# Gathers that wait for the gathers in front of them to be issued

## The chip, the cores and the metric

The kernel runs on one core of one Trainium2 chip. Its five engines are TensorE (PE, the matmuls; PEld is its weight load), VectorE (DVE), ScalarE (ACT), GpSimd (POOL) and SyncE (SP, which here only issues DMAs). The metric is the device time of one launch in microseconds; for a version of the kernel it is the median of several runs without a profiler. A profile is one more execution, taken with the hardware profiler on.

## What is computed

The reference is one layer of a graph network over B = 16 graphs of N = 1024 nodes with C = 64 channels. A node's new value comes from weighted quantiles, per channel, of its neighbours' values. Before that, a node with more than ten neighbours drops some of them.

```python
h = relu(layernorm(x))
neigh = (adj > 0) & ~eye
skip  = where(nb > 10, (nb + 1) // 2, 1)          # nb: number of neighbours
rem   = neigh & (skip > 1) & (rank % skip == skip - 1) & mask
rem   = rem | rem.T
nd    = (adj with its diagonal set, without rem) > 0
s     = sort(where(nd[..., None], h[None], inf), axis=neighbours)
agg   = sum of w * (quantile tau of s)             # tau .25, .5, .75; w .25, .5, .25
out   = h + agg
y     = relu(out @ W1 + b1) @ W2 + b2
x     = x + y * mask
```

The adjacency has about one edge in 128, so a node keeps few neighbours, and the kernel works on lists of them.

## The kernel before

A batch is one graph. `prepare(b)` makes its lists: `load` and `normalize` read the adjacency and the node values from HBM, `drop` and `keep` find on PE and ACT which edges stay, `order` sorts the nodes by their number of neighbours so that nodes with lists of like length lie in the same tile of 128 (eight tiles in four classes with 13, 11, 9 and 7 places), and `collect` leaves, on DVE, the index list `idx` of each tile. `normalize` also writes the node values to a table `htab` in HBM, one row of 64 values for each node.

`fetch(m, classes)` queues the gathers for a pair of batches m. A gather is one indirect DMA that GpSimd issues: for one place s of one tile it reads one index for each of the 128 partitions and brings 128 rows of `htab` to the tile `g` of its class. A pair has 126 of them, the eight pairs 1008; they all stand at line 1199. `fetch_group` adds 26 gathers (L1402) and 4 reads of rows of x (L1406) for the few nodes with long lists, `scatter` 4 indirect writes (L1445).

`aggregate(m)` then sorts the lists in `g` with min and max on DVE (L1236, L1237), weights them (L1244) and adds them up on PE in `acc` (L1246). `mlp` puts the sums in the nodes' order with one-hot matmuls and runs the two layers. `results(m)` is both.

The outer loop runs over m = 0 to 8. In each turn `weave` interleaves `results(m - 1)` with `prepare` for the batches 2m + 2 and 2m + 3 and takes queued gathers out with `issue` as the results advance. The classes with long lists have two buffers for `g`, the other two classes one: their gathers for the next pair can't run until the sums of this one are done.

The order of the program is not the order on the engines. At the end `arrange` takes all instructions, estimates what each costs (a POOL DMA 1330 ns and 950 ns more until its result), lays them out in time with a list schedule, and ties each engine to the order that comes out. Waits between engines are put in afterwards by the framework, one semaphore for each engine; the DMAs that GpSimd issues take eight semaphores in rotation for their completion, and as a rule a gather waits until the one that used its semaphore before has landed. [...] a further wait is put in a semaphore instruction in front of it on the same engine.

The lines that matter below: 1199 (the gather), 639 (`arrange`), 723 (where `arrange` writes the fixed order of each engine), 1175 (the queue and `issue`), 1542 (the call of `arrange`).

Of the kernel before, what the change touches and what calls it, by code (L numbers as in the profile page):

```python
# [635 lines left out]
        return 570, 1700 + by / 200  # L636


def arrange(tc, tails=()):

    steps, found, number = [], {}, {}
    for ins in list(tc.nc.cur_bb.bb.instructions):
        if type(ins).__name__.startswith("BassTile"):
            continue
        if ins.name in tails:
            at = found[tails[ins.name]]
            at.tail.append(ins)
            number[ins.name] = len(number)
            at.busy += Step(ins, 0).busy
            found[ins.name] = at  # L650
            continue
        found[ins.name] = Step(ins, len(steps))
        steps.append(found[ins.name])

    written, read, users, order = {}, {}, {}, {}
    for s in steps:
        for u in s.reads + s.writes:
            name = u.tile.name
            for o, other in written.get(name, ()):
                if u.meets(other):  # L660
                    s.before.add(o.place)
            if u in s.writes:
                for o, other in read.get(name, ()):
                    if u.meets(other):
                        s.before.add(o.place)
        for u in s.writes:
            for table in (written, read):
                table[u.tile.name] = [e for e in table.get(u.tile.name, ()) if not u.covers(e[1])]
            written[u.tile.name].append((s, u))
        for u in s.reads:  # L670
            read.setdefault(u.tile.name, []).append((s, u))
        for u in s.reads + s.writes:
            if getattr(u.tile, "tag", None):
                if u.tile.name not in users:
                    order.setdefault(u.tile.tag, []).append(u.tile)
                users.setdefault(u.tile.name, []).append(s)
    for tiles in order.values():
        for k, t in enumerate(tiles):
            bufs = t.tag_meta.bufs
            first = users[t.name][0]  # L680
            if k:
                first.behind.add(users[tiles[k - 1].name][0].place)
            if k >= bufs:
                first.before.update(o.place for o in users[tiles[k - bufs].name])
            for o in users[t.name][1:]:
                if o is not first:
                    o.before.add(first.place)
    for s in steps:
        s.behind -= s.before
        s.before.discard(s.place)  # L690
        s.behind.discard(s.place)
        s.left, s.ready = len(s.before) + len(s.behind), 0.0
        for p in (*s.before, *s.behind):
            steps[p].after.append(s)

    free = dict.fromkeys(ENGINES, 0.0)
    waiting, able, sequence = ({e: [] for e in ENGINES} for _ in range(3))
    for s in steps:
        if not s.left:
            heappush(waiting[s.engine], (0.0, s.place))  # L700
    for _ in steps:
        when, e = min(
            (free[e] if able[e] else max(free[e], waiting[e][0][0]), e) for e in ENGINES if able[e] or waiting[e]
        )
        while waiting[e] and waiting[e][0][0] <= when:
            heappush(able[e], heappop(waiting[e])[1])
        s = steps[heappop(able[e])]
        sequence[e].append(s)
        free[e] = when + s.busy
        for o in s.after:  # L710
            if s.place in o.behind:
                least = when
            else:
                least = free[e] + (s.lag + 60 if o.engine != e or s.moves else 115 if e == "DVE" else 0)
            o.ready = max(o.ready, least)
            o.left -= 1
            if not o.left:
                heappush(waiting[o.engine], (o.ready, o.place))
        for q in ENGINES:
            while waiting[q] and waiting[q][0][0] <= free[q]:  # L720
                heappush(able[q], heappop(waiting[q])[1])

    for steps in sequence.values():
        alike = iter(sorted((i for s in steps for i in s.tail), key=lambda i: number[i.name]))
        line = [i for s in steps for i in (s.ins, *(next(alike) for _ in s.tail))]
        for ins, then in zip(line, line[1:]):
            tc.add_manual_dep(
                then, ins.name, mybir.DependencyInfo(mybir.DependencyClass.NoSync, mybir.DependencyReason.DATA),
                reason="order of the engine",
            )  # L730
# [3 lines left out]
def list_layer(  # L734
# [14 lines left out]
    nc = tc.nc  # L749
# [420 lines left out]
    tails = {}  # L1170
# [2 lines left out]


    queue = deque()
    turn = [0]

    def issue(many=None):
# [8 lines left out]
    def fetch(m, classes=CLASSES, halves=(0, 1)):  # L1187

        for tiles, slots in classes:
            lo, n = tiles[0], len(tiles)  # L1190
            held, order = PLANS[slots][:2]

            def begin(h, tiles=tiles, lo=lo, n=n, slots=slots, held=held):
                if (m, tiles) not in gathered:
                    gathered[m, tiles] = wk.tile([P, held, n, 2, C], F32, name=f"g{lo}", bufs=2 - lo // 4)
                nc.scalar.copy(gathered[m, tiles][:, slots - 1, :, h], owns[m][:, lo:lo + n, h])

            def gather(h, slot, k, at, tiles=tiles, lo=lo):
                return nc.gpsimd.indirect_dma_start(  # L1199
                    out=gathered[m, tiles][:, slot, k - lo, h], out_offset=None, in_=tables[2 * m + h],  # L1200
                    in_offset=bass.IndirectOffsetOnAxis(ap=lists[2 * m + h][:, at:at + 1], axis=0),
                )

            for h in halves:
                queue.append(partial(begin, h))
                for k in tiles:
                    for s, slot in enumerate(order[:FULL[k] + ((k, FULL[k]) in HOSTS)]):
                        queue.append(partial(gather, h, slot, k, PASSED[k] + s))
# [68 lines left out]
    def aggregate(m, o):  # L1277
# [4 lines left out]
        for half in (0, 1) if last else (1, 0):  # L1282
# [30 lines left out]
            if half and not last:  # L1313
                fetch(m + 1, CLASSES[2:])
# [197 lines left out]
    late_constants()  # L1512
    drain(both(ahead, drop(0), normalize(0)), keep(0), order(0), collect(0, ((0, 1), (1, NT))))
    fetch(0, halves=(0,))
    issue()
    drain(load(1), prepare(1))
    fetch(0, halves=(1,))
    issue()
    for m in range(pairs + 1):
# [19 lines left out]
    fp = psum.tile([1, 1], F32, name="fp", tag="misc")  # L1539
    nc.tensor.matmul(fp, worst, ones_col(cst, nc), start=True, stop=True)  # L1540
    nc.vector.tensor_scalar(flag, fp, 0.0, None, OP.is_gt)
    arrange(tc, tails)


def ones_col(pool, nc):
# [68 lines left out]
@with_exitstack  # L1614
def quantile_graph_layer(
    ctx: ExitStack,
    tc: tile.TileContext,
    x: bass.AP,
    adj: bass.AP,
    nodemask: bass.AP,  # L1620
    W1: bass.AP,
    b1: bass.AP,
    W2: bass.AP,
    b2: bass.AP,
    cbf: bass.AP,
    cf32: bass.AP,
    ci32: bass.AP,
    out: bass.AP,
):
    keep = ctx.enter_context(tc.tile_pool(name="keep", bufs=1))  # L1630
    flag = keep.tile([1, 1], I32, name="flag")
    list_layer(tc, x, adj, nodemask, W1, b1, W2, b2, cbf, cf32, out, flag)
    full = tc.nc.values_load(flag[0:1, 0:1], min_val=0, max_val=1)
    with tc.If(full > 0):
        dense_layer(tc, x, adj, nodemask, W1, b1, W2, b2, cbf, cf32, ci32, out)
# [83 lines left out]
```

## Time and profile before

| | us |
|---|---|
| timed runs, median of 3 | 1597.93 (1597.37 to 1602.03) |
| profiled execution | 2649.33 |
| its span, first to last instruction | 2647.5 |
| PE busy, 8385 matmuls | 1188.3 |
| DVE busy, 3716 instructions | 1183.8 |
| ACT busy, 2510 instructions | 937.0 |
| POOL busy, 1047 instructions | 1029.6 |
| first gather starts / last gather starts | 92.0 / 2441.9 |
| mean granted TensorE clock, share of full speed | 0.69 |

A row of the groups reads: line, engine, operation, output and inputs, count, then busy us and the mean ns of one, then the idle time of the engine just before these instructions and what ended most of it. "issue" is a start that waited for nothing that the trace shows; "remote" is a wait whose releaser the trace does not know. In the timeline a row is start, duration, engine, line, operation, and in brackets the idle time before it. [...] The profiled execution of this kernel takes 1.66 times as long as a timed run, so a share of its span is not a share of the timed run.

### The profile page before, as it was taken

To read this page: it belongs to the slowest core of one execution; us is meant where nothing else is said; L and a number is where in the kernel's file an instruction comes from. 1 tells how busy PE (TensorE), PEld (TensorE's weight loads), DVE (VectorE), ACT (ScalarE), POOL (GpSimd) and SP (SyncE) were. 2 spreads that over 40 slices of the span, in tenths; PEclk is the share of its full clock that TensorE was granted. 3 is DMA by queue.
4 is the path that set the end of the run, shared out by engine and by line. 5 is a ranking of instruction groups with operands and counts; after the bars stand their busy time and mean duration, and the time that the engine had idled before them with its cause. 6 is when DMAs were issued, how large, how long until landed. Compare 5 with 4: busy or idle time off the path is not lost.

```text
span 2647.5 us, 25734 instructions
## 1 busy us (share of the span) xinstructions
PE 1188.3 (45%) x8385; PEld 719.3 (27%) x8385; DVE 1183.8 (45%) x3716; ACT 937.0 (35%) x2510; POOL 1029.6 (39%) x1047
## 2 busy tenths in 40 slices
PE   4427076253807481446616354444942463123235
PEld 2214043132404240223313232232521231021122
DVE  2303066232607460555319323495851452281883
ACT  6528075243607350536225252424631230001001
POOL 0442712744272437252550626307074626406000
PEclk9758577577957695677757676676965676556667
DMA  4323121222222211212111211302220101101000
GB/s 139 92 49 91 41 69 56 60 58 52 50 45 83 54 48 30 77 45 66 34 50 58 52 42 38 84 17 62 53 60 17 31 11 31 28 0 24 16 0 11
DMA packets 151250, 127.47 MB, mean 48 GB/s; under 512 B 117538, under 2 KB 118050, under 8 KB 151106
## 3 DMA queue, kind: packets, MB, share of 16 engines
q1 hardware_dynamic: 117762, 91.52, 12.3%
q0 software_dynamic: 33344, 34.21, 6.7%
q8 instruction: 68, 1.11, 0.2%
q14 instruction: 76, 0.62, 0.1%
HBM read 110.10 MB, written 13.81 MB: 47 GB/s over the span
## 4 chain that ended last, share of the span: by engine, by line
another core or an unknown queue 34%; PE 20%; ACT 16%; DVE 16%; issue 10%; DMA 2%; SPq 1%; DVEq 0%; POOL 0%; POOLq 0%; ACTq 0%
PE codeP L1041 5%; DVE g L1236 3%; DVE g L1237 3%; ACT kept L970 3%; ACT dist L950 3%; ACT sg L866 2%; PE acc L1246 2%; ACT ne L886 2%; PE tp L873 2%; PE rk L940 1%; PE rk L945 1%; DVE gg L1236 1%; DVE gg L1237 1%; ACT waste L1141 1%
## 5 line engine op out<-in xcount | busy, mean ns | idle before, releaser
L1199 POOL DMA_INDIRECT g<-htab,idx x1008 | 995.0, 987 | 1334.5 <-PE acc L1246 424.0
L1236 DVE TENSOR_TENSOR g<-g 128x768 f32<-128x768 f32 (+3 forms) x408 | 281.2, 702 | 60.7 <-remote 29.6
L1237 DVE TENSOR_TENSOR g<-g 128x512 f32<-128x512 f32 (+3 forms) x408 | 282.1, 703 | 33.4 <-PE acc L1287 23.3
L950 ACT ACTIVATE dist<-rk,bias 128x512 f16<-128x512 f32 x256 | 171.0, 695 | 316.9 <-remote 249.0
L873 PE MATMUL tp<-kb,sg 128*128 128x128 bf16 x1024 | 118.1, 262 | 360.9 <-issue 137.5
L886 ACT ACTIVATE ne<-tp 128x512 fp8e4<-128x512 f32 x240 | 137.9, 612 | 355.0 <-remote 303.2
L940 PE MATMUL rk<-kb,cnt 128*128 128x512 bf16 x256 | 126.1, 493 | 300.4 <-issue 153.3
L951 DVE TENSOR_SCALAR rem<-dist,half 128x1024 bf16<-128x1024 f16 x128 | 63.8, 499 | 363.4 <-ACT dist L950 266.6
L1246 PE MATMUL acc<-g,kf 128*128 128x256 f32 (+2 forms) x448 | 145.9, 467 | 162.8 <-DVE pause L1216 98.9
L1041 PE MATMUL codeP<-pack,perm 128*128 128x332 bf16 x1024 | 199.8, 341 | 13.0 <-DVE perm L1016 12.6
L945 PEld LDWEIGHTS <-ne 128*128 128x128 fp8e4 x1024 | 101.3, 120 | 367.0 <-issue 352.3
L873 PEld LDWEIGHTS <-sg 128*128 128x128 bf16 x1024 | 90.7, 120 | 389.1 <-issue 286.5
L970 ACT ACTIVATE kept<-kp 128x512 fp8e4<-128x512 f32 x256 | 151.0, 612 | 92.6 <-remote 70.2
L1246 PEld LDWEIGHTS acc<-g,kf 128*128 128x128 f32 x448 | 90.0, 233 | 191.0 <-DVE pause L1216 104.9
L866 ACT ACTIVATE sg<-at 128x1024 bf16<-128x1024 f32 x128 | 134.0, 1070 | 17.8 <-DMA at<-in_adj_dram 17.2
L945 PE MATMUL rk<-kw,ne 128*128 128x128 fp8e5 x1024 | 133.3, 264 | 0.0
L1380 DVE TENSOR_TENSOR yp<-yp,mask 128x256 f32<-128x256 f32 x32 | 13.7, 429 | 260.9 <-remote 148.3
L1041 PEld LDWEIGHTS <-perm 128*128 128x128 bf16 x1024 | 99.4, 106 | 99.8 <-DVE perm L1016 34.7
L1321 DVE TENSOR_SCALAR at_p<-iota,node 128x512 bf16<-128x512 f16 x256 | 80.1, 362 | 86.8 <-remote 78.3
L973 PE MATMUL code<-kw,kept 128*128 128x17 fp8e5 x1024 | 65.8, 174 | 109.5 <-issue 62.6
L968 PE MATMUL kp<-kw,rem 128*128 128x128 fp8e5 x1024 | 108.9, 233 | 0.0
L963 PE MATMUL kp<-ne,kw 128*128 128x512 fp8e4 x256 | 108.0, 423 | 0.0
(162 smaller groups left out, 2153.8 us busy)
## 6 DMA issues: line engine op xcount, KB each, us to landing
at<-in_adj_dram SPq DMA_DIRECT2D x128, 512.0 KB
g<-htab,idx POOLq DMA_INDIRECT x1008
xt<-in_x_dram SPq DMA_DIRECT2D x16, 256.0 KB
y<-in_x_dram SPq DMA_DIRECT2D x16, 256.0 KB
htab<-xt SPq DMA_DIRECT2D x16, 256.0 KB
gtab<-xt SPq DMA_DIRECT2D x16, 256.0 KB
out_dram<-y SPq DMA_DIRECT2D x16, 256.0 KB
gg<-g SPq DMA_DIRECT2D x32, 48.0 KB
```

What stands on the lines that cost most here:

```text
L866: nc.scalar.activation(sg, at, AF.Sign)
L873: run.append(nc.tensor.matmul(tp[:, s], sg[:, m * P:(m + 1) * P], ident16, start=(s == 0), stop=(s == 3 and t // 4 != n), skip_group_check ...
L886: nc.scalar.activation(to, tp, AF.Relu, saturate=False)
L940: run = [nc.tensor.matmul(rk, cnt[:, ts], blocks[:, 4 * n:4 * n + 4, None].to_broadcast([P, 4, P]), start=True, stop=False, skip_group_che ...
L945: run.append(nc.tensor.matmul(rk[:, s * P:(s + 1) * P], ne[:, 4 * n + s, ts], upper, start=False, stop=(s == 3), skip_group_check=True,))
L950: nc.scalar.activation(dist[:, n * HALF:(n + 1) * HALF], rk, AF.Abs, bias=bias[:, t:t + 1])
L970: nc.scalar.activation(kept[:, 4 * n:4 * n + 4], kp, AF.Relu, saturate=False)
L1041: run.append(nc.tensor.matmul(flat, perm[:, t, k * P:(k + 1) * P], pack[:, t], start=False, stop=(t == NT - 1), skip_group_check=True,))
L1199: return nc.gpsimd.indirect_dma_start(out=gathered[m, tiles][:, slot, k - lo, h], out_offset=None, in_=tables[2 * m + h], in_offset=bass.I ...
L1236: nc.vector.tensor_tensor(at(f, df, n), pa, pb, one)
L1237: ins = nc.vector.tensor_tensor(pa if back else pb, pa, pb, other)
L1246: nc.tensor.matmul(acc, ident32, lines[:, s], start=False, stop=(s == now[-1] and not ends), skip_group_check=True)
```

## The change

Each gather at line 1199 also raises a semaphore of its own, `issued`, from the GpSimd side when it has been issued (not when its data have landed), and its instruction is noted in `given_out`. `arrange`, when GpSimd's order is fixed, goes through the gathers in that order, k = 0, 1, 2, and so on, and gives each with k > 1 a wait until `issued` has reached k - 1: the gathers 0 to k - 2 have been issued, so at most one in front of it is still under way. The gathers of `fetch_group` and the scatters neither raise it nor wait. Nothing else is different: the planner's costs, the order, the buffers and the DMAs are the same.

```diff
-def arrange(tc, tails=()):
+def arrange(tc, tails=(), paced=None):
...
+    if paced:
+        for k, s in enumerate(s for s in sequence["POOL"] if s.ins.name in paced[1]):
+            if k > 1:
+                paced[1][s.ins.name].wait_op(paced[0], k - 1, "sem-ge")
     for steps in sequence.values():
...
     queue = deque()
+    issued, given_out = nc.alloc_semaphore("issued"), {}
     turn = [0]
...
             def gather(h, slot, k, at, tiles=tiles, lo=lo):
-                return nc.gpsimd.indirect_dma_start(
+                ins = nc.gpsimd.indirect_dma_start(
                     out=gathered[m, tiles][:, slot, k - lo, h], out_offset=None, in_=tables[2 * m + h],
                     in_offset=bass.IndirectOffsetOnAxis(ap=lists[2 * m + h][:, at:at + 1], axis=0),
+                    engine_sem=issued,
                 )
+                given_out[ins.ins.name] = ins
+                return ins
...
-    arrange(tc, tails)
+    arrange(tc, tails, (issued, given_out))
```

## The prediction

> **What bounds the kernel now.** I read the page's engine table first, then the tile view of the gathers' source, then busy time by stretches, then two pieces of the timeline.
>
> ```profile
> span 2647.5 us, 25734 instructions
> PE 1188.3 (45%) x8385; PEld 719.3 (27%) x8385; DVE 1183.8 (45%) x3716; ACT 937.0 (35%) x2510; POOL 1029.6 (39%) x1047
> L1199 POOL DMA_INDIRECT g<-htab,idx x1008 | 995.0, 987 | 1334.5 <-PE acc L1246 424.0
> ```
>
> No engine is busy for half of the span. What strikes first is that the profiled execution took 2649.33 us (span 2647.5, so 1.8 around it), while the median of the timed runs is 1597.93. The trace is 1051 us longer than the run that is judged, so I must say which part of the trace the timed run has. The tile view of the table that is gathered from:
>
> ```profile
> L1199 POOL DMA_INDIRECT g<-htab,idx x1008: 941/947/3896, 92.0 to 2441.9; - x168
>   issue: 294.5, 966
>   DMA g<-htab,idx: 5.5, 18
>   POOL g L1199: 5.5, 18
> ```
>
> Half of the gathers take 947 ns or less, and 966 of 1008 start 294.5 / 966 = 0.30 us after the one in front with nothing to wait for: 1.25 us from start to start. Only 18 were put down to another gather's DMA. Now the stretches (columns: stretch, length, busy us and count on PE, PEld, DVE, ACT, POOL, granted clock, DMA share, GB/s):
>
> ```profile
> 92.00:171.00 79.00, 10.22 (x87) 5.83 (x85) 10.10 (x52) 13.05 (x31) 60.10 (x63) 0.55 0.26 58
> 171.00:247.00 76.00, 53.33 (x495) 34.86 (x494) 23.88 (x102) 60.73 (x159) 0.14 (x1) 0.84 0.29 89
> 1008.00:1078.00 70.00, 6.05 (x32) 4.05 (x32) 2.06 (x5) 2.83 (x4) 52.93 (x57) 0.52 0.16 33
> 1078.00:1145.00 67.00, 43.67 (x405) 28.76 (x405) 52.52 (x137) 44.85 (x116) 0.70 (x2) 0.82 0.30 85
> ```
>
> While GpSimd streams gathers, the rest of the core nearly stands still (PE 6 us in 70); when the stream ends, it runs. Over all 22 streams and the 25 stretches between them the same view adds up to:
>
> ```profile
> sum 1336.60, PE 378.36 PEld 213.41 DVE 329.44 ACT 278.16 POOL 1025.76; mean PE 17.20 PEld 9.70 DVE 14.97 ACT 12.64 POOL 46.63
> sum 1308.90, PE 809.95 PEld 505.86 DVE 854.32 ACT 658.88 POOL 1.90; mean PE 32.40 PEld 20.23 DVE 34.17 ACT 26.36 POOL 0.08
> ```
>
> In the streams PE is 28% busy and DVE 25%; between them 62% and 65%. The timed run does the same work in 1597.9 us: 1188.3 / 1597.9 = 74% on PE, 74% on DVE. That is denser than even the stretches without gathers. Such standstills can't be in the timed run at anything like this size: they belong to the profiled execution. What bounds the timed run is PE and DVE together. Between 1078 and 1367 (one pair of batches) PE has 137.9 us of work and DVE 131.3; six full stages of this kind, a start of 92 us and a tail of 192 us without gathers, and the stages that fill and empty the pipeline leave little air in 1598 (the sum stands at rival 3).
>
> Last, what the others wait for in a stream and at its end:
>
> ```profile
> 1004.93 0.69 ACT L1362 ACTIVATE h<-hp,b1c 128x512 f32<-128x512 f32 x1 [12.67 <-remote]
> 1049.72 0.69 ACT L950 ACTIVATE dist<-rk,bias 128x512 f16<-128x512 f32 x1 [44.10 <-remote]
> ...
> 1077.47 0.95 POOL L1199 DMA_INDIRECT g<-htab,idx  x1 [0.30 <-issue]
> 1088.23 0.69 ACT L950 ACTIVATE dist<-rk,bias 128x512 f16<-128x512 f32 x1 [12.47 <-remote]
> ```
>
> ACT waits up to 44 us for matmuls that the trace starts long before, and is let go 10 us after the last gather has ended. GpSimd meanwhile keeps its 1.25 us.
>
> [...]
>
> **The change, part by part.**
>
> (a) The new semaphore: one raise at each of 1008 gathers. The trace has no gather with it. Lower bound 0, upper bound 0.05 us on GpSimd (three of the 17 ns semaphore instructions). I take 0.
>
> (b) The wait: gather k waits until gather k-2 has been issued. Most gathers wait already, for the completion semaphore that comes round every eight gathers, so nearly each of 1006 gets one more semaphore instruction in front: 17 ns by the L1199 row. [...] It lies beside the running gather's 0.947 us and costs nothing[...].
>
> (c) Does the wait hold a gather back? From release to start: the first gather starts at 91.98 after its index list is done at 91.70, 0.28 us. Gather k-2 ends; k-1 starts 0.30 later and runs 0.95; k could start 0.30 after that, 1.55 us after k-2 ended. Released by a semaphore that arrives L after that end, it can start at L + 0.28. It is late only if L is above 1.27 us. [...] Cost 0. What stands behind a waiting gather on GpSimd are the next gathers, the 30 gathers for the group and the 4 scatters; behind them wait the sorts (L1236, L1237) and their accumulations. None moves if no gather starts later.
>
> (d) What it could take away: the queue of ready gathers is at most two deep[...]. The rate of gathers stays 1.25 us, and with it whatever piles up at each gather.
>
> (e) Order of instructions: the planner in `arrange` sees no new cost, the waits are put in after the order is fixed. All engines keep their order. No buffer, DMA or size changes.
>
> Sum: 0 + 0 + 0 on the path. Against the profiled execution's own time that is 2649 again; against the timed median 1597.93 I forecast 1598. I apply the sum of zero to both, and no ratio between them is needed.
>
> **The rivals.**
>
> 1. No change, 1598, own range 1593 to 1603. [...] Against: GpSimd streams for 1042 x 1.25 = 1303 us, 82% of the timed run if it keeps that pace there, so it is no idle engine and small costs may show.
>
> 2. Slower, by one mechanism: the hand-over between gathers gets onto GpSimd's path at L1199. Its small end is (a) at 0.02 us for each gather: 1008 x 0.02 = 20 us, half of it hidden where GpSimd waits anyway (424 us for `acc`, L1246): 1608. Its large end is a semaphore that is raised only when the data have landed. The period is then (0.95 + L + 0.28) / 2; [...] It decides from L = 1.27 on[...]. For it: a wait is added and none is taken away. Against: 0.30 us between gathers whether the next one is queued or not.
>
> 3. Faster: ready gathers in the queue, not their rate, hold up PE, and the timed run has a little of it. Bound: six full stages at PE's 138 us, the start (92), the second batch (76), the first pair (2 x 76), the last-but-one results (DVE's rows L1236, L1237, L1244, L1233, L1321: 750 / 8 = 94) and the tail (192) make 1434 if everything overlapped perfectly, so 164 us is the ceiling; a sixth of it gives 1571. For it: the standstills sit exactly in the streams. Against: in the stream from 838 on, PE does 28.8 us in 65, though gathers are queued from its first microsecond, and after a stream's end PE is still late by 10 us with no gather queued. Both speak for something that fills with the number of gathers, which this change leaves alone.
>
> 4. The change doesn't do what it says: the lane waits had limited the queue already and the new wait is never last. The time is that of rival 1; it is counted there.
>
> **How the numbers follow.** About 0.3% (5 us) is what a measurement of this kernel tells from no change. Rival 1 with 4: 0.45. Slower: 0.35, nearer its small end. Faster: 0.20. The likeliest is 1598. For 8 in 10 I go down to 1570 (rival 3's 1571) and up to 1638[...].
>
> **What would show it.** In the trace of the changed kernel: some 1000 more semaphore instructions on GpSimd at L1199; gathers in streams still 1.25 us apart (c); if they are 1.3 or more, rival 2 runs. If the span stays near 2650, the standstill follows the rate of gathers (d); if it falls by hundreds of us, it followed the queue, and rival 3 gains, but only the timed runs say whether they had any of it. I am wrong if the timed median leaves 1593 to 1603 and the gathers' period has not moved.

## The result, and the profile after

The changed kernel takes 1603.09 us in the median of 20 runs (1600.23 to 1610.36), the kernel before, timed beside it, 1599.83 (1595.74 to 1604.44). The ratio is 1.0022 with a 95% interval of 1.0012 to 1.0032: 3.3 us more, at the edge of what can be told from no change.

The two traces can't be set against each other without one remark. Of the chips that these runs came to, some take about 1,600 us for the kernel before (the first kind, below), others about 2,660 us (the second kind), timed and profiled alike. The profile of before is of the second kind, while its timed runs, the result and the profile after are of the first. Below, a time is only compared with one of the same kind, and trace readings say which kind they are from.

The profile page after (first kind), the lines that answer to those of before, with the busy tenths of GpSimd's row in 40 slices:

```profile
span 1599.7 us, 26689 instructions
PE 1087.4 (68%) x8385; PEld 676.0 (42%) x8385; DVE 1185.7 (74%) x3716; ACT 922.8 (58%) x2510; POOL 1117.7 (70%) x1047
...
POOL 0057777577777777777877777777777777777830
...
L1204 POOL DMA_INDIRECT g<-htab,idx x1008 | 1081.3, 1073 | 411.4 <-DMA g<-htab,idx 300.5
```

There are 955 more instructions (26689 against 25734), the semaphore instructions in front of the gathers. The gathers' line is now 1204. What matters most is the POOL row: it stands at 7, but for one 5 and two 8s, from the fourth slice to the thirty-eighth. That looks like a quarter of air, but it is none, because a gather of 0.95 us is followed by 0.30 us until the next one starts, the hand-over, which isn't counted as busy: 0.95 / 1.25 = 0.76. A 7 is GpSimd issuing gathers one after the other. The tile view of the gathered table and GpSimd's list of waits (columns: us in total, times, longest us) say the same:

```profile
L1204 POOL DMA_INDIRECT g<-htab,idx x1008: 940/948/3650, 93.3 to 1536.6; - x168
```

```profile
POOL g L1204 <- DMA g<-htab,idx: 300.5, 977, 0.8
POOL g L1204 <- DVE idx L1089: 91.4, 1, 91.4
POOL out_dram L1453 <- issue: 50.4, 3, 49.8
POOL g L1204 <- issue: 12.4, 7, 9.7
```

The first gather starts at 93.3 us, the last ends at 1537.5, and between them GpSimd waits for another engine for about 10 us in all. The 977 waits of 0.31 us in the mean are put down to another gather's DMA, but they are the same 0.30 us that the trace of before called "issue"; the longest is 0.8. The last 890 indirect DMAs up to there, the group's 30 and two scatters among them, run without a break from 301.6 to 1537.5: 1235.9 / 890 = 1.389 us each. The busy time in this stretch (columns as in the prediction):

```profile
302.00:1537.00 1235.00, 845.45 (x6358) 524.46 (x6358) 1012.42 (x3113) 672.33 (x1837) 961.54 (x890) 0.83 0.28 73
```

PE is busy for 68% of it and DVE for 82%, more than GpSimd's 78%. But GpSimd's 961.5 us and 889 hand-overs of 0.305 us make 1233 of 1235, while DVE has real pauses: of its 218 idle us there, 207 lie in 158 waits of over 0.1 us, most of them for ACT (139.5 us). In this execution the line of gathers sets the end. The trace before, with GpSimd idle for 424 us until `acc` came, couldn't show it.

### The profile page after: what moved, and what is told of

It reads as the page before. It is cut to its first block, busy times and chain, and to the rows that moved or that the text cites. A ratio compares the mean times of both kernels' runs of the same rounds, so it can differ in the third digit from the quotient of the medians.

```text
span 1599.7 us, 26689 instructions
## 1 busy us (share of the span) xinstructions
PE 1087.4 (68%) x8385; PEld 676.0 (42%) x8385; DVE 1185.7 (74%) x3716; ACT 922.8 (58%) x2510; POOL 1117.7 (70%) x1047
## 5 line engine op out<-in xcount | busy, mean ns | idle before, releaser
L1204 POOL DMA_INDIRECT g<-htab,idx x1008 | 1081.3, 1073 | 411.4 <-DMA g<-htab,idx 300.5
L1244 DVE TENSOR_TENSOR g<-g 128x768 f32<-128x768 f32 (+3 forms) x408 | 281.3, 702 | 39.2 <-DMA g<-htab,idx 33.2
L1245 DVE TENSOR_TENSOR g<-g 128x512 f32<-128x512 f32 (+3 forms) x408 | 282.1, 703 | 10.2 <-DMA gg<-g 6.7
L1045 PE MATMUL codeP<-pack,perm 128*128 128x332 bf16 x1024 | 186.3, 325 | 18.5 <-DVE perm L1020 18.4
L877 PE MATMUL tp<-kb,sg 128*128 128x128 bf16 x1024 | 112.0, 253 | 89.7 <-ACT sg L870 65.8
L944 PE MATMUL rk<-kb,cnt 128*128 128x512 bf16 x256 | 118.0, 461 | 46.2 <-ACT dist L954 41.7
L949 PEld LDWEIGHTS <-ne 128*128 128x128 fp8e4 x1024 | 94.9, 114 | 104.6 <-issue 84.7
L949 PE MATMUL rk<-kw,ne 128*128 128x128 fp8e5 x1024 | 124.0, 250 | 0.0
L972 PE MATMUL kp<-kw,rem 128*128 128x128 fp8e5 x1024 | 99.3, 218 | 0.0
L967 PE MATMUL kp<-ne,kw 128*128 128x512 fp8e4 x256 | 97.8, 383 | 0.0
L968 PE MATMUL kp<-rem,kw 128*128 128x512 bf16 x256 | 96.9, 379 | 0.0
L1050 ACT CAST st<-codeP 128x4 bf16<-128x4 f32 x128 | 21.1, 165 | 124.8 <-PE codeP L1045 123.8
```

The source lines that it names most:

```text
L877: run.append(nc.tensor.matmul(tp[:, s], sg[:, m * P:(m + 1) * P], ident16, start=(s == 0), stop=(s == 3 and t // 4 != n), skip_group_check ...
L944: run = [nc.tensor.matmul(rk, cnt[:, ts], blocks[:, 4 * n:4 * n + 4, None].to_broadcast([P, 4, P]), start=True, stop=False, skip_group_che ...
L949: run.append(nc.tensor.matmul(rk[:, s * P:(s + 1) * P], ne[:, 4 * n + s, ts], upper, start=False, stop=(s == 3), skip_group_check=True,))
L1045: run.append(nc.tensor.matmul(flat, perm[:, t, k * P:(k + 1) * P], pack[:, t], start=False, stop=(t == NT - 1), skip_group_check=True,))
L1204: ins = nc.gpsimd.indirect_dma_start(out=gathered[m, tiles][:, slot, k - lo, h], out_offset=None, in_=tables[2 * m + h], in_offset=bass.In ...
L1244: nc.vector.tensor_tensor(at(f, df, n), pa, pb, one)
```

## The experiments

Theory G: GpSimd's line of gathers sets the end of a run that takes about 1,600 us. Theory F: the 3.3 us come from single gathers that the short queue lets start late. A kernel is called n deep when a gather waits until all but the last n - 1 in front of it have been issued: the change is two deep. Rivals: P, PE and DVE set the end, as the prediction had it; the raises or the extra instructions cost something by themselves. About the standstill of the profile before, theory Q: it follows the depth of the queue of ready gathers.

### The depth of the queue: raises alone, one, four and six deep

From the changed kernel, raises alone (e1):

```diff
-    arrange(tc, tails, (issued, given_out))
+    arrange(tc, tails)
```

and all in front waited for, which is one deep (e2); e3 and e4 have `k > 3` with `k - 3` and `k > 5` with `k - 5` in these two lines:

```diff
-            if k > 1:
-                paced[1][s.ins.name].wait_op(paced[0], k - 1, "sem-ge")
+            if k > 0:
+                paced[1][s.ins.name].wait_op(paced[0], k, "sem-ge")
```

> Each gather raises the semaphore, and nothing waits for it. Theory Q (the depth of the queue of ready gathers makes the standstill of the profiled execution, not the raises): the profiled span stays near 2650 us, as before the change. Rival (the engine's own raise at each gather alters how the execution is recorded): span near 1600. Timed, theory F (the extra time of the change comes from the waits, which leave the queue at most two deep and so uncover what happens between two gathers): 1599 to 1600 us, ratio 1.000 within 0.001. Rival R (the raise itself costs): 1603 us, ratio 1.002.

> A gather waits until every gather in front has been issued, so the hand-over stands bare between each two. Theory G (GpSimd's line of gathers sets the end of a timed run): the 0.305 us between two gathers grows by the hand-over, 0.05 to 0.3 us each, and the run by 890 to 1040 times that, so 1650 to 1900 us; the change of the run follows the gap nearly one for one. Rival P (PE and DVE together set the end, as the prediction had it): under a third of that, 1610 to 1640 us. Profiled span as the timed run in either case, no standstill.

> As the change, but a gather waits until all but the last three in front have been issued, so up to four stand in the queue. Theory F (a hiccup at every 106th gather is uncovered by the short queue): the late gathers vanish and the time is that of before, ratio 0.999 to 1.001. Rival (the extra instructions in front of the gathers cost by themselves): 1.002 as with the change. The profiled span tells at which depth the standstill comes: near 1600 if four gathers don't yet hold up the others' completions, near 2650 if they do.

> As the change, but all but the last five in front, so up to six stand in the queue. Theory Q: the standstill of the profiled execution grows with the depth, so a span between that of four deep and 2650 us, most likely above 2000. Rival (any wait between gathers ends it): near 1600. Timed: ratio 0.999 to 1.001 by theory F.

The chip was one of the second kind: before took 2666.49 us. Medians were 2663.05, 2657.39, 2683.54 and 2683.93, ratios 0.987 (0.979 to 0.995, from few runs), 0.995 (0.993 to 0.998), 1.008 (1.005 to 1.010) and 1.009 (1.006 to 1.011). The kernel of e2, run again on another such chip (e5 below), gave 1.002 (1.000 to 1.004), so half a per cent there is no reading. From the page of e2:

```profile
span 2639.6 us, 26689 instructions
PE 1170.2 (44%) x8385; PEld 711.8 (27%) x8385; DVE 1180.7 (45%) x3716; ACT 935.7 (35%) x2510; POOL 1026.1 (39%) x1047
...
POOL 0441712645271527342460525407075627406000
```

This is nearly the POOL row of the page before (0442712744272437252550626307074626406000), streams and pauses in turn. The spans are 2670, 2640, 2681 and 2689 us for raises alone, one, four and six deep. Theory Q falls: a queue of one has the standstill in full. And the change does not take it away; the profile after is free of it because it was taken on a chip of the first kind. The same kernel as e2 on that kind (e9 below) shows what is different: ACT's waits of over 0.1 us whose releaser the trace doesn't know come to 948 us in e2's trace, and e9's has none.

For theory F, the traces of e2 to e4 already tell something. With all in front waited for, nine gathers start 2.0 to 2.1 us after the end of the one in front instead of 0.305. Numbered from 0 through all 1042 indirect DMAs of GpSimd, the group's and the scatters too, they are 113, 219, 325 and so on to 961, exactly every 106th. Within the streams the gaps of all others are still 0.305, so the 0.05 to 0.3 us for each gather that theory G was given for e2 don't come. Four and six deep have none at these numbers. The trace of the change itself (first kind) has eight of them, at the same numbers (855 is missing), 0.46 to 0.83 us after the end of the one in front.

### One deep, timed again

> The kernel of the second run again, to be timed where the kernel before takes about 1600 us. In its trace above the gaps between two gathers stayed at 0.305 us but for some thirty of about 2.1 us, one at every few dozen gathers. Theory G (GpSimd's line of gathers sets the end of such a run): each of those adds about 1.8 us to the line, so 20 to 60 us in all, 1620 to 1660 us. Rival P (PE and DVE set the end): within 0.4 % of before, under 1606 us.

A chip of the second kind again: 2699.36 us against 2693.14, ratio 1.002. Its trace repeats the nine breaks at the same gathers; the question of the time stayed open.

### More gathers

From the kernel before:

```diff
                 for k in tiles:
+                    queue.append(partial(gather, h, order[FULL[k] - 1], k, PASSED[k]))
                     for s, slot in enumerate(order[:FULL[k] + ((k, FULL[k]) in HOSTS)]):
```

> The kernel before, with 128 more gathers (one for each half and tile of each pair, a second fetch of a row that is overwritten by the real one), which the kernel's planner places among the others. Where the kernel before takes about 1600 us: theory G (GpSimd's line of gathers sets the end) gives 128 x 1.25 to 1.39 us = 160 to 178 us more, about 1760 to 1780 us; rival P (PE and DVE set it, GpSimd has room) gives under 40 us more, 1600 to 1640 us. Where before takes about 2660 us instead: if the standstill follows the gathers, 0.12 x 1050 us = some 130 us more, about 2790 us; if PE alone makes it, under 30 us more.

On a chip of the second kind: 3003.4 us against 2664.02, ratio 1.129 (1.120 to 1.138). 339 us for 128 gathers are 2.65 us each, more than twice their own 1.25, and more than the 130 us that I had expected if the standstill follows them. A stretch with gathers and the one after it:

```profile
1077.00:1187.00 110.00, 24.40 (x104) 14.05 (x103) 12.34 (x39) 8.48 (x17) 83.01 (x87) 0.58 0.17 34
1188.00:1300.00 112.00, 70.53 (x570) 46.28 (x570) 94.49 (x272) 70.74 (x174) 0.06 (x1) 0.76 0.23 69
```

There the core does mostly either gathers or the rest (PE 24 us of 110 beside them, 71 of 112 without), so that a gather's time is added in full or more; why, no run here shows. The planner also reorders the other engines around the added gathers, which is part of the 339 us.

### Three deep

From the changed kernel:

```diff
-            if k > 1:
-                paced[1][s.ins.name].wait_op(paced[0], k - 1, "sem-ge")
+            if k > 2:
+                paced[1][s.ins.name].wait_op(paced[0], k - 2, "sem-ge")
```

> As the change, but a gather waits until all but the last two in front have been issued, so three may stand in the queue. With all in front waited for, some thirty gathers came 1.8 us late; with the change's two in the queue a gather's 1.25 us hide most of it, and its trace has nine gathers late by 0.15 to 0.53 us. Theory F: a third gather in the queue hides the rest, no gap between gathers of one stream above 0.32 us, and where before takes about 1600 us the time is that of before, ratio 0.999 to 1.001. Rival (the extra semaphore instructions or the raises cost by themselves): late gathers stay or not, ratio 1.002 as with the change. Where before takes about 2660 us, only the gaps can be read.

First kind: 1596.99 us (1593.12 to 1602.76) against 1598.48, ratio 1.0002 (0.9986 to 1.0018). This kernel has every raise and every extra instruction of the change, and one gather more in the queue. The late gathers are gone. What makes them late is still there: three deep, GpSimd's semaphore instructions pause nine times for 3.1 us, each time just ahead of one of the nine gathers (from 392.16 to 395.24 us here), but the gathers already in the queue run on meanwhile. The same gather in the timeline of GpSimd, first three deep, then the change, then one deep (e9 below):

```profile
394.91 0.94 POOL L1204 DMA_INDIRECT g<-htab,idx  x1 [0.30 <-DMA g<-htab,idx]
396.16 0.94 POOL L1204 DMA_INDIRECT g<-htab,idx  x1 [0.30 <-DMA g<-htab,idx]
```

```profile
394.19 0.95 POOL L1204 DMA_INDIRECT g<-htab,idx  x1 [0.30 <-DMA g<-htab,idx]
395.97 1.08 POOL L1204 DMA_INDIRECT g<-htab,idx  x1 [0.83 <-DMA g<-htab,idx]
```

```profile
391.77 1.07 POOL L1204 DMA_INDIRECT g<-htab,idx  x1 [0.30 <-DMA g<-htab,idx]
394.81 1.17 POOL L1204 DMA_INDIRECT g<-htab,idx  x1 [1.96 <-issue]
```

So the raises and the extra instructions cost nothing that this can measure, and theory F holds in the trace: 0.30, 0.83 and 1.96 us in front of the second gather. The intervals of three deep and of the change overlap between 1.0012 and 1.0018, so the times alone would not settle it.

### More gathers and one deep, on a chip of the first kind

> The kernel of the sixth run again (128 more gathers), to be timed where the kernel before takes about 1600 us. Theory G (GpSimd's line of gathers sets the end of such a run): 128 x 1.25 to 1.39 us = 160 to 178 us more, 1760 to 1780 us, with no break of over 15 us in the gathers between 300 us and the last. Rival P (PE and DVE set it): under 40 us more, 1600 to 1640 us.

> The kernel of the second and fifth run again (a gather waits for all in front), to be timed where the kernel before takes about 1600 us. Theory F with G: about ten to thirty gathers come 1.8 us late each and the others not at all, so 15 to 55 us more, 1615 to 1655 us. Rival: the others' late gathers were only the ends of streams, so 0.2 to 0.4 % more, like the change, 1602 to 1606 us; rival P: as before, 1598 to 1602 us.

The kernel of e6 took 1771.53 us against 1600.81, ratio 1.107 (1.104 to 1.110): 171 us, 1.33 us for each added gather, within theory G's 160 to 178 and far from rival P's 40. Lines of its page and of its waits:

```profile
span 1772.4 us, 26002 instructions
PE 1096.1 (62%) x8385; PEld 684.8 (39%) x8385; DVE 1207.6 (68%) x3716; ACT 931.0 (53%) x2510; POOL 1258.6 (71%) x1175
...
POOL 0067776777777788777777778777777787777840
```

```profile
POOL g L1199 <- issue: 322.4, 1058, 0.3
POOL g L1199 <- DMA gtab<-xt: 90.6, 1, 90.6
```

The shares of PE and DVE are six points lower than in the profile after while the run is longer; GpSimd's stays at 70 to 71%, and its row is again one of sevens. That is what a bound looks like. The planner's order for the other engines is different here too, but the line leaves little for it to do. From GpSimd's last wait, 6.6 us long, to the end of the line at 1709.9, 1013 indirect DMAs run without a break in 1404.5 us, 1.386 us each, against 890 in 1235.9 us, 1.389 each, in the trace after. The line is 169 us longer, and the run 171.

The kernel of e2 and e5 took 1610.61 us, ratio 1.0079 (1.0051 to 1.0106), so 12.6 us more (8 to 17). That is under the expected 15 to 55, which only the interval's upper end reaches, since I had taken the ends of streams on the second kind for late gathers: the trace has nine of these, not thirty. Both rivals fall, as no run of it took less than 1608.03 us. The nine lie 14.7 us above nine gaps of 0.305. The first comes before GpSimd's last wait for another engine, which can swallow it (5.1 us here, 8.9 three deep); the other eight make 12.9 us. The same sum over the change's eight is 2.8 us, 2.5 without the first, where 3.3 (1.9 to 5.1) were measured. Two depths, two sums, both within the measured interval: as theory G has it, a late gather in the unbroken line moves the end by what it is late.

### What comes every 106 gathers

From one deep, a semaphore instruction behind each gather, which the planner counts at nothing:

```diff
...
                 given_out[ins.ins.name] = ins
+                tails[nc.gpsimd.sem_inc(passed).ins.name] = ins.ins.name
```

> All in front waited for, as in the ninth run, with one more semaphore instruction on GpSimd behind each gather: three instructions for a gather instead of two. In the ninth run a gather came about 1.6 us late at every 106th, which is every 212th instruction. Theory I[...]: the breaks come at every 71st gather (212 / 3), so about 14 instead of 9, each as long as before, on any chip. Rival D (something that counts gathers[...]): they stay at every 106th. Where before takes about 1600 us, theory I gives 8 us more than the ninth run, 1616 to 1622 us.

Theory I, that the breaks go by the number of GpSimd's instructions, falls. With half as many instructions more, breaks of 2.0 to 2.2 us are still at 113, 219, 537, 643, 749, 855 and 961, and longer ones of 3.75 and 4.04 us at 325 and 431 (a timeline of GpSimd, second kind, around 219):

```profile
586.92 0.94 POOL L1205 DMA_INDIRECT g<-htab,idx  x1 [0.30 <-issue]
590.04 0.94 POOL L1205 DMA_INDIRECT g<-htab,idx  x1 [2.18 <-issue]
```

It is something that goes by the count of GpSimd's indirect DMAs, ahead of their execution: three deep it holds back semaphore instructions, nine times for 3.1 us, and no gather. What it is stays open. Over a hundred other gathers came late in this run, in groups and up to 2.6 us after the end of the one in front, which no theory had foreseen and which I can't explain; the run's time, 0.979 of before's on this chip, is one of the readings of the second kind that I don't use.

### More work on DVE

From the kernel before, with a tile `spent` that is set to zero at the start:

```diff
     def let_go(held, ins):
         if held < 0.8:
             return held
+        nc.vector.tensor_tensor(spent, spent, spent, OP.min)
```

> The kernel before, with 578 more operations on DVE (a minimum of a tile of 128 x 64 f32 with itself, one ahead of each pause)[...]; their result is used by nothing. Where before takes about 1600 us: theory G (GpSimd's line sets the end) gives only what gathers are lengthened beside a busy DVE[...], so 1610 to 1630 us. Rival P (PE and DVE set it): [...]1650 to 1680 us. Where before takes about 2660 us: the same two, no more can be read.

Inconclusive. The operations took 0.225 us each in the median, 130 us in all, but depended on nothing and so were placed in the first 677 us, and the chip was of the second kind: ratio 1.001 (0.999 to 1.003). By how much DVE could be loaded on the first kind before it sets the end was not measured; the 207 us of waits in the trace after are all there is on it.

### Half gathers

From the kernel with more gathers:

```diff
-                    queue.append(partial(gather, h, order[FULL[k] - 1], k, PASSED[k]))
+                    queue.append(partial(gather, h, order[FULL[k] - 1], k, PASSED[k], P // 2))
```

(`gather` takes the number of partitions for the destination and for the indices.)

> The kernel of the eighth run, with its 128 more gathers over 64 partitions instead of 128 (the order of the others is the same). It measures what a gather's time is made of. If rows set it[...]: the extra ones take 0.47 to 0.6 us beside the others' 0.95, and where before takes about 1600 us the run is 128 x (0.5 + 0.305) = 103 us longer than before, about 1700 us. If a gather has a fixed price: 0.9 to 0.95 us each and 171 us longer, as the eighth run. With rival P (GpSimd has room) the eighth run's 171 us would not have come about; a time that follows the extra gathers' length a second time strengthens theory G.

Second kind: 3022.86 us against 2691.41, ratio 1.122 (1.117 to 1.126), so its time can't be set beside e8's 171 us. The durations can be read. In GpSimd's timeline the third row is a half gather:

```profile
107.51 0.95 POOL L1199 DMA_INDIRECT g<-htab,idx  x1 [0.30 <-issue]
108.76 0.94 POOL L1199 DMA_INDIRECT g<-htab,idx  x1 [0.30 <-issue]
110.01 0.92 POOL L1199 DMA_INDIRECT g<-htab,idx  x1 [0.30 <-issue]
```

Over all 128 the median is 0.917 us, against 0.947 for a full one. Half the rows save 0.03 us: between 64 and 128 rows a gather has a nearly fixed price.

## Why the prediction was right, and where it wasn't

The forecast of no change at 1598 us held: 1603.09, ratio 1.0022, within the 0.3% that it named. Its sum of zero rests on (a) to (c) and not on what bounds the kernel, so the number is not luck; what it missed stands at (b) and (c). But it was not right for all of its reasons.

**What bounds the kernel: wrong.** "What bounds the timed run is PE and DVE together" is the step that failed. GpSimd does: 171 us for 128 more gathers. The number for it stood in rival 1, GpSimd streaming for 1042 x 1.25 = 1303 us, 82% of the timed run. I took it for a warning, since the trace had GpSimd idle for 61% of the span and waiting for `acc` for 424 us. But those waits were part of the standstill that I had just set aside as not of the timed run. What was missing is that gathers are longer when the other engines work beside them, 1.073 us in the mean after against 0.987 before; with the hand-over, the 1040 indirect DMAs up to 1537.5 us make 1040 x 1.378 = 1433 us, and with 93 us until the first one starts, about 10 of waits and 62 after the last the sum is 1598 of a span of 1599.7. The wrong bound also stood in rival 2, which took half of a cost as hidden in GpSimd's waits for `acc`: with about 10 us of waits in the trace after there was nothing to hide in, and one deep shows its late gathers in full.

**Standstill: half right.** It is not in the timed run that the result is measured with, as the prediction said. That it belongs to the profiled execution is wrong: on a chip of the second kind the timed runs take as long (2666 us), and on one of the first the profiled execution of the change took 1601.47 us, in the midst of its timed runs. Recording alone doesn't make it.

**(a): right. (b): right where a gather covers it, and short where none does.** The row of the semaphore instructions that (a) and (b) went by, in the trace of before:

```profile
L1199 POOLq EVENT_SEMAPHORE  x87: 17/17/90205, 44.9 to 2413.7; - x87
```

Three deep has every raise and every extra instruction, at 1.0002. Where no running gather covers them, though, the extra instructions show. The gather at 150 waits for its index list; it starts 0.74 us after the list is done in the traces of the change, three deep and e9, and the gather that waits for it in e8, without the change, starts after 0.27. The second kind has the same at gather 252 after PE's `acc`: 0.27 us before and with raises alone, 0.74 in e2 to e4. That is 0.47 us for an instruction whose row shows 17 ns in the median. On the first kind GpSimd has only one or two such waits, so it comes to half a microsecond or one; with the 2.5 us of the late gathers in the line it makes 3.0 of the 3.3.

**(c): right for a gather, short by one term.** A gather is late from L = 1.27 us on. No trace had shown L before the result: that it lies below was my estimate, and so was how far rival 2's large end reaches, on which the 1638 of the range leaned. Now even one deep nearly all gaps stay at 0.305 us, so a hand-over by the semaphore fits into the 0.30 that was there before. With the 0.28 us from release to start that (c) read, this leaves about 0.03 us for L, an estimate from these two numbers. With this rival 2's large end falls, a raise only when the data have landed: in e9's trace a gather's last data packet ends 1.2 us after its row in the median, four times as late as the next gather starts (in the trace after 1.13 us). Not foreseen was what comes every 106 gathers: eight times 0.15 to 0.53 us above the usual gap, 2.8 us. The place is rival 2's, the gap between gathers on GpSimd's path, at a seventh of the 20 us of its small end and at eight gathers rather than all. These eight, which three deep doesn't have, also rule out rival 4: the new wait is sometimes last.

**(d) fell as a test.** A span that falls by hundreds of us was to mean that the standstill followed the queue. The span did fall, by 1048 us, and it meant neither queue nor rate: with raises alone and one, four and six deep, all stand still on one kind of chip, and on the other neither the change nor one or three deep does, nor e8, which has nothing of it. Rival 3, which would have gained by that reading, had no ground. The sign for rival 2, gathers 1.3 us apart or more, would have misled too: they are 1.389 us apart in the line after, but 1.386 in e8's, without the change. The gathers are longer there, not the gaps. That timed runs alone decide what is gained was right.

**(e): right.** In the traces before and after, PE, ACT and GpSimd run the same operations on the same tiles in the same order. DVE's records differ in 20 pairs of neighbours, each time a memset of `pause` and the operation beside it, which start within 25 ns of each other in one of the traces.

## What to carry to other kernels

Count an engine's time with its hand-overs: a row of sevens, or 70% busy, was a full engine here, and DVE with 74% was not, since each 0.95 us gather brings 0.30 us that no row counts. When the profiled execution is far from the timed one, don't read idle times from it, not even for the engine that seems to wait most; add up issue time per engine instead and compare it with the timed run. And when a queue is made short on the engine that sets the end, expect to pay for rare events that the queue had covered: three gathers deep cost nothing that could be measured, two 3.3 us, one 12.6.

## What the runs showed of the hardware

- Gathers and the rest of the core nearly exclude each other on some chips and not on others: beside a stream of gathers PE is busy for 24 us of 110 in e6 and for 845 of 1235 in the trace after. The kernel before takes 2664 to 2693 us on the four that e1 to e6 and e10 to e12 came to, and 1598 to 1601 on the two of e7 to e9. The cause is open, also whether it is the chip or a state that it was in.
- At every 106th indirect DMA of GpSimd something takes about 1.6 us ahead of execution (gaps of 1.74 to 2.10 us one deep in e9). Three deep GpSimd's semaphore instructions pause for 3.1 us in the same nine places, and no gather is late. It doesn't go by the number of instructions: with half as many more (e10) the breaks are at the same nine gathers.
- A gather of 64 rows takes 0.917 us, one of 128 rows 0.947: half the rows save 0.03 us, while 128 more gathers cost 1.33 us each where GpSimd's line sets the end (e8).
- In the trace after, the 122 gathers with nothing on DVE beside them take 0.945 us in the mean, the 218 with the sort's min and max (L1244, L1245) for over nine tenths of their time 1.15, and the 168 with as much other work of DVE and none of these 1.03. So a gather beside these fp32 operations is longer by a fifth. The cause was not tested.
